# Selective scan with four states of 32 channels on the partitions, one broadcast of B for three groups, and part of the product with B on GpSimd

## The chip, the cores and the metric

One core of a Trainium2 chip. The metric is the device time of one launch in microseconds, and each kernel ran several times on the same chip as runs of the kernel before. A ratio here is the mean time of one kernel's fast runs over the mean of the other's fast runs of the same rounds, so it is not quite the ratio of the medians that are quoted beside it.

## The reference, cut to what matters

Four blocks work on images of 4 x 56 x 56 x 96. The first two contain a selective scan over the 3136 pixels of an image, in four directions, for 192 channels with 16 states each. The scans take nearly all of the time. Everything else (norms, projections, convolutions, attention, feed-forward) is called side work below, because the kernels run it beside the scans.

```python
dt = softplus(dt_raw @ dtw + dtb)            # (l, 192)
d_a = exp(dt[..., None] * a)                 # (l, 192, 16)
d_b = dt[..., None] * b_ssm[:, :, None, :]   # B is shared by the channels
h = d_a * h + d_b * x[..., None]             # the scan along l
y = einsum('bds,bs->bd', h, c_ssm)           # C is shared by the channels
```

## The kernel before

A direction's pixels are cut into 4 steps of 784 columns. That makes 2 layers x 4 images x 4 directions x 4 steps = 128 chunks. Before the change the 128 partitions hold 64 channels for two states, and a unit is one of 3 channel groups and one of 8 pairs of states. TensorE broadcasts B to the partitions into PSUM; VectorE multiplies dt*u by it **in place in PSUM** and scans; GpSimd multiplies by C; TensorE sums over the states.

```python
da = sp.tile([128, CS], F32, name="da", bufs=3)
nc.scalar.activation(da, ch.dt[g], AF.Exp, scale=ch.na[:, g, q : q + 1])
db = b                                              # B, broadcast, in PSUM
nc.vector.tensor_tensor(db, ch.du[g], db, ALU.mult)  # the product stays in PSUM
if n + 1 < len(units):
    b = self.spread_b(units[n + 1][0], units[n + 1][2])
...
hs = sp.tile([128, CS], F32, name="hs", bufs=2)
nc.vector.tensor_tensor_scan(
    hs[:, way], da[:, way], db[:, way], at if ch.step else 0.0, ALU.mult, ALU.add
)
...
hc = sp.tile([128, CS], F32, name="hc", bufs=2)
nc.gpsimd.tensor_tensor(hc, hs, ch.cc[q // 2][:, q % 2], ALU.mult)
```

The side work is written as generators from which the scan loop takes pieces at its yields. And the program text is not the order of the queues: a scheduler reorders the instructions of each engine at build time, by its own model of their durations, and each engine then works through its queue in that order.

## Time and profile before

| | before |
|---|---|
| time, median (range) | 12832 us (12782 to 12865, 4 runs of the comparison below) |
| TensorE / VectorE / GpSimd busy | 83% / 70% / 54% |
| scans, a unit | 1.84 us, never above 1.850 us |
| read and written by the DMA queue | 654 MB, 20.6% of the engines' time |

The lines themselves, and the pace of a unit worked out from them, are in the prediction. An engine whose work for one unit is far shorter than the pace is waiting for something.

### The profile page before, as it was taken

The page shows a single profiled execution, that of the slowest core. Times are in us where ns is not written, and L with a number is a line of the kernel's source. Part 1 is how long each engine was busy: PE and PEld are TensorE (multiplying, and loading weights), DVE is VectorE, ACT ScalarE, POOL GpSimd, SP SyncE. Part 2 cuts the span into 40 slices and gives each one's busy share as a digit, 9 for nine tenths or more (in the row PEclk, how much of TensorE's full clock was granted, in tenths as well). Part 3 has the DMA queues.
Part 4 walks back from the last instruction along what each step waited for, and adds up shares of the span by engine and source line. Part 5 has one row for each costly group of instructions (what it writes and reads, how often), then busy time and mean ns, then how long its engine had stood idle before and what let it go on. Part 6 is the DMA issues. An engine that isn't in the chain of part 4 may idle for free. (4 is left out here: it accounts for less than half of the span.)

```text
span 12868.3 us, 101763 instructions
## 1 busy us (share of the span) xinstructions
PE 10724.2 (83%) x32510; PEld 3416.3 (27%) x32510; DVE 9010.8 (70%) x7546; ACT 6582.8 (51%) x10422; POOL 6985.7 (54%) x3964
## 2 busy tenths in 40 slices
PE   7888888987789878897889888888888888888786
PEld 3222122222223122231223223321233213332143
DVE  4776777667776777767776666877668776777722
ACT  4655555555555555555555544445444454445511
POOL 4555656556554665546555555556555565555510
PEclk6766667766667667776767677766777667776665
DMA  3221212112211221212222121211212122211110
GB/s 84 61 59 46 69 45 54 49 41 68 57 48 50 57 67 42 57 44 65 50 54 53 37 68 49 52 45 41 62 49 52 41 50 61 51 43 40 41 33 28
DMA packets 233374, 662.64 MB, mean 51 GB/s; under 512 B 60866, under 2 KB 141252, under 8 KB 231204
## 3 DMA queue, kind: packets, MB, share of 16 engines
q1 hardware_dynamic: 232064, 654.32, 20.6%
q8 instruction: 257, 4.21, 0.1%
q14 instruction: 281, 2.30, 0.1%
q10 hardware_dynamic: 772, 1.80, 0.1%
HBM read 548.41 MB, written 107.58 MB: 51 GB/s over the span
## 5 line engine op out<-in xcount | busy, mean ns | idle before, releaser
L537 POOL TENSOR_TENSOR hc<-hs,cc 128x784 f32<-128x784 f32 x3072 | 5704.9, 1870 | 4545.8 <-DVE hs L531 3550.0
L551 PE MATMUL y<-hc,two 128*64 128x392 f32 x12288 | 4120.3, 740 | 1294.4 <-POOL hc L537 1219.0
L524 DVE TENSOR_TENSOR b<-du,b 128x784 f32<-128x784 f32 x3072 | 2963.4, 970 | 2481.5 <-PE b L483 2468.6
L531 DVE TENSOR_TENSOR_SCAN hs<-da,carry,b 128x784 f32<-128x784 f32 x2304 | 4166.1, 1834 | 149.4 <-ACT da L522 91.7
L522 ACT ACTIVATE da<-dt,na 128x784 f32<-128x784 f32 x3072 | 2862.0, 945 | 728.9 <-DVE hs L531 714.1
L483 PE MATMUL b<-bc,sel 96*128 96x512 bf16 (+1 forms) x6144 | 2110.7, 436 | 489.9 <-DVE hs L531 486.3
L551 PEld LDWEIGHTS y<-hc,two 128*64 128x64 f32 x12288 | 839.8, 178 | 3117.3 <-POOL hc L537 2320.1
L535 ACT COPY carry<-hs 128x1 f32<-128x1 f32 x2304 | 431.8, 189 | 2140.9 <-DVE hs L531 2134.1
L531 DVE TENSOR_TENSOR_SCAN hs<-da,b 128x784 f32<-128x784 f32 x768 | 1346.3, 1774 | 54.4 <-ACT da L522 21.5
L483 PEld LDWEIGHTS <-sel 96*128 96x128 bf16 x6144 | 457.7, 108 | 3176.4 <-DVE hs L531 1322.1
L431 PE MATMUL ps<-U,wd 64*108 64x392 f32 (+1 forms) x1536 | 864.0, 774 | 0.0
L461 POOL TENSOR_TENSOR du<-dt,U 128x784 f32<-128x784 f32 x384 | 783.0, 2047 | 147.0 <-ACT dt L456 138.9
L593 POOL TENSOR_TENSOR rs<-rs,power 112x4 f32<-112x4 f32 x252 | 257.4, 1021 | 964.6 <-ACT rs L592 784.8
L455 PE MATMUL ps<-dtr,wd 12*128 12x392 f32 (+1 forms) x1536 | 752.5, 736 | 9.4 <-ACT dt L456 3.6
L652 PE MATMUL ps<-win,dg 64*64 64x220 f32 (+9 forms) x2016 | 689.5, 496 | 0.0
L522 ACT ACT_TABLE_LOAD x511 | 655.6, 1283 | 8.3
L568 ACT COPY Ya<-y 64x392 f32<-64x392 f32 x512 | 348.3, 680 | 550.8 <-PE y L565 476.6
L596 PE MATMUL ps<-ident,rs 112*96 112x112 f32 x2016 | 423.6, 376 | 202.8 <-POOL rs L593 202.0
L456 ACT ACTIVATE dt<-ps,wd 128x392 f32<-128x392 f32 x768 | 426.8, 585 | 288.8 <-PE ps L455 279.7
L456 ACT ACT_TABLE_LOAD x339 | 434.9, 1283 | 78.9 <-PE ps L455 73.7
L596 PEld LDWEIGHTS ps<-ident,rs 112*96 112x96 f32 x2016 | 349.2, 250 | 395.4 <-POOL rs L593 308.0
L652 PEld LDWEIGHTS ps<-win,dg 64*64 64x64 f32 (+2 forms) x2016 | 337.1, 175 | 353.9 <-issue 258.7
(215 smaller groups left out, 6739.9 us busy)
## 6 DMA issues: line engine op xcount, KB each, us to landing
cc<-cd SPq DMA_DIRECT2D x1024, 392.0 KB, 5.2
U<-u SPq DMA_DIRECT2D x64, 588.0 KB, 7.9
u<-w SPq DMA_DIRECT2D x56, 224.0 KB, 2.8
z<-w SPq DMA_DIRECT2D x56, 224.0 KB, 2.7
y<-Ya SPq DMA_DIRECT2D x8, 1568.0 KB, 7.0
w<-y SPq DMA_DIRECT2D x56, 224.0 KB, 3.9
w<-z SPq DMA_DIRECT2D x56, 224.0 KB, 4.0
wd<-in_wd_dram SPq DMA_DIRECT2D x32, 367.5 KB, 3.5
```

Of the source, the lines that this page charges most:

```text
L431: nc.tensor.matmul(ps[:m, :HC].rearrange("p (a b) -> p a b", b=HS), self.wx[rows, g, :m], self.in_order(self.U[rows, g], orient, c * CS + ...
L455: nc.tensor.matmul(ps[:, :HC], wt[rows, g], dtr[rows], start=True, stop=True)
L456: nc.scalar.activation(dt[:, h * HC : (h + 1) * HC], ps[:, :HC], AF.Softplus, bias=dtb[:, g : g + 1])
L461: nc.gpsimd.tensor_tensor(du.rearrange("p (a b) -> p a b", b=HS), ch.dt[g].rearrange("p (a b) -> p a b", b=HS), self.in_order(self.U[:, g] ...
L483: self.nc.tensor.matmul(ps[:, s], w, ch.bc[:, s], start=True, stop=True)
L522: nc.scalar.activation(da, ch.dt[g], AF.Exp, scale=ch.na[:, g, q : q + 1])
L524: nc.vector.tensor_tensor(db, ch.du[g], db, ALU.mult)
L531: nc.vector.tensor_tensor_scan(hs[:, way], da[:, way], db[:, way], at if ch.step else 0.0, ALU.mult, ALU.add)
L537: nc.gpsimd.tensor_tensor(hc, hs, ch.cc[q // 2][:, q % 2], ALU.mult)
L551: nc.tensor.matmul(self.y[64 * h : 64 * h + 64, :HC], self.two, hc[:, h * HC : (h + 1) * HC], start=q == 0, stop=False,)
L596: nc.tensor.matmul(ps[:, b], rs[:, q : q + 1].to_broadcast([NT, C]), self.ident[:NT, :NT], start=True, stop=True)
L652: self.nc.tensor.matmul(o[:, a - r0 : e - r0, x0:x1], diag[:, tap], win[:, a + dy - lo : e + dy - lo, x0 + dx : x1 + dx], start=n == 0, st ...
```

## The change

The intent: with four states of 32 channels on the partitions, one broadcast of B serves three channel groups, which relieves TensorE, the fullest engine. One of the three products with B goes from VectorE to GpSimd, and the product with C becomes one wide instruction. Since a channel's dt must now stand on four partition blocks, dt and dt*u are written to DRAM and read back four times.

```diff
@@ spread: new @@
+        for n, l in ((0, ch.dt), (1, ch.du)):
+            t = self.sp.tile([128, NG, CS], F32, name="dt" if n == 0 else "du")
+            for s in range(4):
+                self.nc.sync.dma_start(
+                    t[32 * s : 32 * s + 32], ch.dd[e][n].rearrange("(g d) t -> d g t", d=32)
+                )
+            l.append(t)
@@ spread_b: f32, one for three groups, and a copy to SBUF for GpSimd @@
+        ps = self.psum.tile([128, 2, 512], F32, tag="b", name="b", bufs=1)
+        for h in range(2):
+            nc.tensor.matmul(ps[:, h, :HC], self.sel[:, h, q], ch.cf, start=True, stop=True)
+        b = self.sp.tile([128, CS], F32, name="bs", bufs=1)
+        nc.scalar.copy(b.rearrange("p (h t) -> p h t", h=2), ps[:, :, :HC])
@@ begin(n): the third group's product with B, a round ahead @@
+            b, bs = self.spread_b(ch, q)
+            v = sp.tile([128, NG, CS], F32, name="v", bufs=3)
+            nc.gpsimd.tensor_tensor(v[:, 2], ch.du[e][:, 2], bs, ALU.mult)
@@ a round @@
-            db = b
-            nc.vector.tensor_tensor(db, ch.du[g], db, ALU.mult)
+                if g < 2:
+                    nc.vector.tensor_tensor(
+                        v[:, g].rearrange("p (h t) -> p h t", h=2),
+                        ch.du[e][:, g].rearrange("p (h t) -> p h t", h=2), b, ALU.mult,
+                    )
+            if n + 1 < len(rounds):
+                nxt = begin(n + 1)
...
-            nc.vector.tensor_tensor_scan(
-                hs[:, way], da[:, way], db[:, way], at if ch.step else 0.0, ALU.mult, ALU.add
-            )
+            for g in range(NG):
+                nc.vector.tensor_tensor_scan(
+                    v[:, g, way], das[g][:, way], v[:, g, way], at[:, g : g + 1] if ch.step else 0.0, ALU.mult, ALU.add
+                )
...
-            nc.gpsimd.tensor_tensor(hc, hs, ch.cc[q // 2][:, q % 2], ALU.mult)
+            nc.gpsimd.tensor_tensor(v, v, cc.unsqueeze(1).to_broadcast([128, NG, CS]), ALU.mult)
```

Cut: the new layout of the parameters, the projections (a third fewer matmuls), the sums over four states in column blocks of 32, the convolutions split into pieces of three taps, and tile counts. A chunk now has 8 rounds (2 halves of 96 channels x 4 groups of states), numbered 0 to 7 below; there are 1024 rounds.

## The prediction

> **What bounds the kernel now.** I read the page's busy shares first, then the costliest groups and the waits.
>
> ```profile
> PE 10724.2 (83%) x32510; PEld 3416.3 (27%) x32510; DVE 9010.8 (70%) x7546; ACT 6582.8 (51%) x10422; POOL 6985.7 (54%) x3964
> ...
> L537 POOL TENSOR_TENSOR hc<-hs,cc 128x784 f32<-128x784 f32 x3072 | 5704.9, 1870 | 4545.8 <-DVE hs L531 3550.0
> L551 PE MATMUL y<-hc,two 128*64 128x392 f32 x12288 | 4120.3, 740 | 1294.4 <-POOL hc L537 1219.0
> L524 DVE TENSOR_TENSOR b<-du,b 128x784 f32<-128x784 f32 x3072 | 2963.4, 970 | 2481.5 <-PE b L483 2468.6
> L531 DVE TENSOR_TENSOR_SCAN hs<-da,carry,b 128x784 f32<-128x784 f32 x2304 | 4166.1, 1834 | 149.4 <-ACT da L522 91.7
> ```
>
> There are 3072 units (128 chunks x 24), each one product with B, one scan, one product with C. TensorE is the fullest engine. VectorE, next in line, is idle for 2481 us before its product with B, nearly all of it for the broadcast of B out of TensorE (2468.6). So TensorE's in-order stream paces VectorE. The chain of waits that ended last covers too little of the span to say more. In the table by stage, the stretch from 150 to 12275 us holds the scans (6908 us of GpSimd, 8885 us of VectorE); 150 us lie before it and 593 us after it. A unit thus takes 12125 / 3072 = 3.95 us, three units 11.84 us.
>
> The third view decides this case: least, median and greatest duration of single lines of VectorE.
>
> ```profile
> L531 DVE TENSOR_TENSOR_SCAN hs<-da,carry,b x2304: 1811/1839/1850, 235.2 to 12272.6; 128x784 f32<-128x784 f32 x192
> L815 DVE TENSOR_TENSOR w<-w,ps x28: 591/618/619, 7594.1 to 12564.8; 96x448 f32<-96x448 f32 x28
> L862 DVE TENSOR_TENSOR w<-w,yq x56: 587/610/2991, 8031.0 to 12863.1; 96x448 f32<-96x448 f32 x56
> L818 DVE SCALAR_TENSOR_TENSOR w<-w,c,win x28: 654/656/4555, 7596.3 to 12565.5; 96x448 f32<-96x448 f32 x28
> ```
>
> The scan now reads one operand from SBUF (da) and one from PSUM (the product with B stays in its PSUM bank): it never varies. L815 also has a PSUM operand, and never varies. L862 and L818 read two tensors from SBUF, and are stretched up to sevenfold. The timeline around the longest:
>
> ```profile
> 11051.87 1.01 POOL L593 TENSOR_TENSOR rs<-rs,power 112x4 f32<-112x4 f32 x1 [5.12 <-ACT rs L592]
> 11052.45 4.55 DVE L818 SCALAR_TENSOR_TENSOR w<-w,c,win 96x448 f32<-96x448 f32 x1
> 11052.84 3.68 POOL L537 TENSOR_TENSOR hc<-hs,cc 128x784 f32<-128x784 f32 x2
> ```
>
> VectorE began at 11052.45 while GpSimd worked, and ended at 11057.00, 0.48 us after GpSimd's third instruction (11056.52). So a 0.66 us instruction sat out two whole products with C. GpSimd kept the resource from one instruction to the next.
>
> **What the Trainium skill says.** "SBUF — State Buffer", section "Who interferes with whom": a VectorE instruction with two SBUF inputs contends with a GpSimd instruction that reads SBUF; whoever comes first has the shared port for the whole instruction. The trace agrees (4.55 against 0.66 us; and one-SBUF-input scans at 1850 ns at most). "GPSIMD Engine Reference", section 3.1 gives 4497 ns for a two-input product of 2048 columns; the trace has 1862 ns (median) for 784, so the slope is (4497 - 1862) / 1264 = 2.085 ns a column. "TensorE: Matmul & The Clock Gate", Part 3, says matmuls with disjoint 32-column outputs run side by side; the trace has this for two of 64 (12288 at a mean of 740 ns are 4120 us busy, 335 each).
>
> **The change, part by part.** A round is now three units that share one B: 1024 rounds.
>
> TensorE is relieved. Broadcast: two f32 matmuls of 392 columns a round, against six bf16 ones (2680 us by the groups with shapes kept apart, busy union 2111). A 392-column f32 matmul takes about 0.75 us, so 1024 x 2 x 0.75 = 1536 us. Summing over states: 6 matmuls of 32 outputs a round, three side by side, 2 x 0.7 us a round: about 1430 us against 4120. Projections and step sizes: a third of the instructions, saving about 1000 us. TensorE falls from 10.7 to about 6.5 ms and no longer paces anything.
>
> VectorE: one of three products with B goes, 1024 x 0.97 = -990 us; some 140 us of remainders for the bf16 split go too. ScalarE: +1024 copies of B to SBUF at some 0.9 us (two of 392 columns take 0.47 each), minus two of three carry copies (-290 us), minus a third of the softplus and several casts: about level, 51% today, not a bound. DMA: dt and dt*u spread over DRAM, 128 chunks x 16 transfers x 301 KB = 616 MB on top of 663. At today's 20.6% share for 654 MB that makes some 40%; a transfer of 392 KB lands in 5.2 us, and each spread has two to three rounds of over 10 us: hidden.
>
> The part that costs: the product with B now lands in an SBUF tile v, because GpSimd cannot use PSUM and v is later multiplied whole. So **the scan reads da and v, two SBUF tensors**, and falls into the class of L862 and L818. GpSimd's reads and all scans then take turns. What needs the port, per round:
> - Product with C, now one instruction of 2352 columns: 1.862 + 1568 x 0.002085 = 5.13 us (an estimate with the page's slope; by three of today's it would be 5.59).
> - Product of one group with B on GpSimd: 784 columns, 1.86 us.
> - dt*u: 256 at 2.047 us (L461, 384 today) = 524 us, 0.51 a round. The small powers (L593): 252 x 1.02 us, some 0.22 a round within the scans.
> - Three scans: (4166 + 1346) us of both scan rows / 3072 = 1.79 each, 5.38 us.
> - VectorE's other instructions with two SBUF inputs, or of the 16-bit kind that L853 and L854 show stretched as well: at their medians about 0.18 ms, 0.18 a round.
>
> Sum: 5.13 + 1.86 + 0.51 + 0.22 + 5.38 + 0.18 = 13.3 us. The two products left on VectorE (1.94 us) have a PSUM input and run beside the product with C. I add 0.5 us a round for moments when neither holds the port: VectorE's side instructions that lie between scans (about 0.25 ms in all) and its waits for side chains (100 to 147 us for each of five lines in the list of waits: L797, L809, L686, L888, L845), some now on the path. Handing over is about even: a released VectorE instruction ends 0.48 us after GpSimd where it takes 0.61 to 0.66 alone, and GpSimd starts 0.14 us after a scan ends.
>
> 13.8 us x 1024 = 14.13 ms, plus 0.15 ms ahead and 0.59 ms behind, which hardly change: 14.87 ms. I say 14800 us, 15% slower, though VectorE and TensorE both have less to do.
>
> **The rivals.**
> 1. No lock for scans: the engines overlap as before. Then VectorE has 1024 x (1.94 + 5.38) + 570 us of the rest = 8.1 ms and GpSimd 1024 x 7.0 + 0.75 ms = 7.9 ms, nearly balanced, TensorE out of the way: with a tenth of waits and 0.74 ms of ends some 9.3 to 9.9 ms, 25% faster. This is what the change aims at. Against it: every line with two SBUF inputs in the trace shows stretched cases, including plain float ones. For it: no scan with two SBUF inputs exists in this trace, and a scan takes 2.3 ns a column, so it might leave the port free half of the time.
> 2. A partial lock, with the port shared by columns or released between scans in a useful way: something between, 11 to 12.7 ms. Against it: the 4.55 us case is whole instructions, and both orders show it: in the timeline the product with C that starts at 11208.30, 0.22 us behind an L862, takes 2.13 us against a median of 1.86.
> 3. Lock plus convoys: GpSimd's in-order queue holds powers and dt*u that wait for ScalarE (today 785 us for L592) while a scan waits behind the port; or the spread through DRAM arrives late at the chunk's start. Each 1 us a round is 1.0 ms: 15.5 to 16.5 ms. For it: nothing overlaps any more, so side waits count. Against it: TensorE has slack now, so side chains get shorter.
>
> **Range and chances.** The mechanism is the large doubt, its size the small one. Given the lock, the sum runs from 13.8 (no extra, cheap handovers) to 15.6 ms (5.59 us products with C, 1.3 us lost a round). No lock or a weak one: 8% together for faster. Between them, 3%. Slower: 89%. Range 13800 to 15700.
>
> **What would show it.** Right: scans with a mean well over 1.84 us, up to some 7 or 8 us for the first scan of a round, or with medians unchanged but long maxima; GpSimd and VectorE hardly ever at work together save in the products with B; the wide product with C near 5.1 us when it isn't blocked; TensorE under 60% busy and no wait for L483's successor worth a millisecond; DMA landing well ahead of use. Wrong: scans steady at 1.84 us with GpSimd busy beside them, and a span under 10 ms (rival 1); a wide product near 5.6 us; ScalarE or the spread named as the releaser of the scans (rival 3).

## The result, and the profile after

After: 16251 us median (16239 to 16265, 4 runs), before: 12832 us. Ratio 1.267 (95% interval 1.262 to 1.272): slower, by more than the range allowed.

The page of the kernel after: busy time of each engine, and groups by line (busy us, mean ns of one, idle time before them and its releaser).

```profile
PE 9331.0 (57%) x28926; PEld 3524.1 (22%) x28926; DVE 12472.7 (77%) x6273; ACT 5527.1 (34%) x7879; POOL 9309.0 (57%) x2680
...
L560 DVE TENSOR_TENSOR_SCAN v<-da,carry,v 128x784 f32<-128x784 f32 x2304 | 7524.0, 3315 | 175.3 <-ACT da L548 149.0
L568 POOL TENSOR_TENSOR v<-v,cc 128x2352 f32<-128x2352 f32 x1024 | 5923.6, 5786 | 352.1 <-ACT carry L566 226.0
```

TensorE was relieved as intended and is no longer the fullest engine. But a scan takes 3315 ns in the mean instead of 1834. Single lines of the kernel after, least / median / greatest duration in ns:

```profile
L560 DVE TENSOR_TENSOR_SCAN v<-da,carry,v x2304: 1812/1840/11820, 262.4 to 15622.2; 128x784 f32<-128x784 f32 x192
L568 POOL TENSOR_TENSOR v<-v,cc x1024: 5122/5160/11188, 156.9 to 15624.1; 128x2352 f32<-128x2352 f32 x171
L551 DVE TENSOR_TENSOR v<-du,b x2048: 934/961/973, 149.7 to 15608.1; 128x784 f32<-128x784 f32 x187
```

The scan's median is unchanged and its greatest value is over six times that; the product with B on VectorE, which has one input in PSUM, never varies. The timeline of one round shows how the two engines stand in each other's way (start, duration, engine, line):

```profile
7211.55 1.85 DVE L551 TENSOR_TENSOR v<-du,b 128x784 f32<-128x784 f32 x2 [1.81 <-ACT bs L485]
...
7213.32 10.10 DVE L560 TENSOR_TENSOR_SCAN v<-da,v 128x784 f32<-128x784 f32 x3
7213.46 6.63 POOL L568 TENSOR_TENSOR v<-v,cc 128x2352 f32<-128x2352 f32 x1
```

Three scans that take 5.3 us alone took 10.10, and the product with C took 6.63 instead of 5.16. The sum of the four alone would be 10.5 us: they ran one after the other. Taken singly in the trace, the scans are 1.83, 6.67 and 1.76 us long. The product with C started during the first and ended 4.94 us after it. The second scan started when the first ended and was done only 1.65 us after the product with C.

How far does this explain the time? From the starts and ends in the trace I took, within the stretch of the scans (15472 us), the time in which an instruction of GpSimd or a scan of VectorE is open, and the rest. The port is the access to SBUF for which the two engines take turns (see the prediction); an instruction that has started and waits for it counts as open.

| stage of the scans | after | a round |
|---|---|---|
| GpSimd's instruction or a scan open | 12900 us | 12.6 us (the prediction's sum: 13.3) |
| neither | 2572 us | 2.5 us (the prediction: 0.5) |

(The prediction's 13.3 holds 0.18 us of VectorE's other instructions, which are not counted here.) So the lock, that is the taking of turns, cost about what was predicted, even a little less, and the excess over the prediction is idle time that was to be 0.5 us a round. It isn't even over the rounds. The gap between the starts of successive products with C, median over 128 chunks, from round r to r+1:

| r | 0 | 1 | 2 | 3 | 4 | 5 | 6 | 7 |
|---|---|---|---|---|---|---|---|---|
| after, us | 14.2 | **20.2** | 14.0 | 11.7 | 11.9 | 12.7 | 13.4 | 13.9 |

One gap in each chunk is 8 us too long (its mean, 25.1 us, is longer still). The timeline of the kernel after around such a gap:

```profile
1917.81 11.72 DVE L560 TENSOR_TENSOR_SCAN v<-da,carry,v 128x784 f32<-128x784 f32 x3
1917.89 6.71 POOL L568 TENSOR_TENSOR v<-v,cc 128x2352 f32<-128x2352 f32 x1
...
1924.55 3.33 POOL L521 TENSOR_TENSOR v<-du,bs 128x784 f32<-128x784 f32 x1
...
1929.45 1.82 DVE L551 TENSOR_TENSOR v<-du,b 128x784 f32<-128x784 f32 x2
...
1931.42 2.95 PE L483 MATMUL b<-cf,sel 128*128 128x392 f32 x4 [3.94 <-DVE v L551]
1934.47 0.81 ACT L485 COPY bs<-b 128x784 f32<-128x784 f32 x1 [3.95 <-PE b L483]
...
1935.36 2.81 POOL L521 TENSOR_TENSOR v<-du,bs 128x784 f32<-128x784 f32 x1 [7.47 <-DMA U<-u]
...
1938.13 5.14 POOL L568 TENSOR_TENSOR v<-v,cc 128x2352 f32<-128x2352 f32 x1
```

The scans that the product with C at 1938.13 needs ended at 1929.53. But in GpSimd's queue two products with B (L521) stand before it. The second waits for a copy of B (1934.47), that for a broadcast (1931.42), that for the PSUM tile to come free (VectorE's products at 1929.45). GpSimd is idle for 7.47 us, and for the last 5.8 of them the product with C was ready behind the head of its queue. (The view names a transfer as the releaser because that came last by its record; the chain just read goes through the copy.)

### The profile page after: what moved, and what is told of

The parts are those of the page before. It is cut to its first block, busy times and chain, and to the rows that moved or that the text cites. A ratio compares the mean times of both kernels' runs of the same rounds, so it can differ in the third digit from the quotient of the medians.

```text
span 16237.4 us, 95405 instructions
## 1 busy us (share of the span) xinstructions
PE 9331.0 (57%) x28926; PEld 3524.1 (22%) x28926; DVE 12472.7 (77%) x6273; ACT 5527.1 (34%) x7879; POOL 9309.0 (57%) x2680
## 3 DMA queue, kind: packets, MB, share of 16 engines
q1 hardware_dynamic: 631424, 1399.75, 34.5%
## 5 line engine op out<-in xcount | busy, mean ns | idle before, releaser
L560 DVE TENSOR_TENSOR_SCAN v<-da,carry,v 128x784 f32<-128x784 f32 x2304 | 7524.0, 3315 | 175.3 <-ACT da L548 149.0
L568 POOL TENSOR_TENSOR v<-v,cc 128x2352 f32<-128x2352 f32 x1024 | 5923.6, 5786 | 352.1 <-ACT carry L566 226.0
L521 POOL TENSOR_TENSOR v<-du,bs 128x784 f32<-128x784 f32 x1024 | 2358.3, 2303 | 4048.4 <-ACT bs L485 2819.8
L583 PE MATMUL y<-v,four 128*32 128x392 f32 x12288 | 2753.2, 756 | 2864.4 <-POOL v L568 2247.9
L483 PE MATMUL b<-cf,sel 128*128 128x392 f32 x4096 | 2612.6, 780 | 2507.0 <-DVE v L551 2506.2
L551 DVE TENSOR_TENSOR v<-du,b 128x784 f32<-128x784 f32 x2048 | 1884.9, 959 | 1616.8 <-ACT bs L485 727.9
L560 DVE TENSOR_TENSOR_SCAN v<-da,v 128x784 f32<-128x784 f32 x768 | 2516.9, 3326 | 73.4 <-ACT da L548 73.4
L483 PEld LDWEIGHTS b<-cf,sel 128*128 128x128 f32 x4096 | 1066.4, 286 | 4074.0 <-issue 3817.9
L485 ACT COPY bs<-b 128x784 f32<-128x784 f32 x1024 | 822.3, 803 | 1087.7 <-PE b L483 1062.5
L453 POOL TENSOR_TENSOR duc<-dtc,U 96x784 f32<-96x784 f32 x256 | 669.8, 2616 | 662.4 <-ACT dtc L443 448.4
```

What stands on the lines that cost most here:

```text
L453: nc.gpsimd.tensor_tensor(du.rearrange("p (a b) -> p a b", b=HS), ch.dtc[e].rearrange("p (a b) -> p a b", b=HS), self.in_order(self.U[e], ...
L483: nc.tensor.matmul(ps[:, h, :HC], self.sel[:, h, q], ch.cf, start=True, stop=True)
L485: nc.scalar.copy(b.rearrange("p (h t) -> p h t", h=2), ps[:, :, :HC])
L521: nc.gpsimd.tensor_tensor(v[:, 2], ch.du[e][:, 2], bs, ALU.mult)
L551: nc.vector.tensor_tensor(v[:, g].rearrange("p (h t) -> p h t", h=2), ch.du[e][:, g].rearrange("p (h t) -> p h t", h=2), b, ALU.mult,)
L560: nc.vector.tensor_tensor_scan(v[:, g, way], das[g][:, way], v[:, g, way], at[:, g : g + 1] if ch.step else 0.0, ALU.mult, ALU.add)
```

## The experiments

Three theories of the result were at stake from the start: the lock (the scan's second operand in SBUF), the convoys (side chains in GpSimd's queue), and, against the prediction's word "hidden", the spread through DRAM. In the diffs "kernel after" is the base unless another is named; they are cut, and some draw several lines together. Six runs compute something else on purpose (e6, e10, e11, e13, e15, e18). They passed the comparison with the reference all the same; its tolerance evidently doesn't see what they leave out, so they count only for their times, and passing does not by itself prove the other runs right.

### e1 and e2: only the operand's place

```diff
+  p = self.psum.tile([128, 1024], F32, tag="p", name="p", bufs=1)[:, :CS]   # e1
+  p = sp.tile([128, CS], F32, name="p", bufs=1)                             # e2
   nc.vector.tensor_tensor(p, ch.du[e][:, g], b, ALU.mult)     # all three groups on VectorE
-  nc.vector.tensor_tensor_scan(v[:, g, way], das[g][:, way], v[:, g, way], ...)
+  nc.vector.tensor_tensor_scan(v[:, g, way], das[g][:, way], p[:, way], ...)
   # no copy of B; convolutions whole and two ps tiles instead of four, to make room in PSUM
```

> Keeps four states of 32 channels, the single broadcast of B and the spread via DRAM; all three products with B go back to VectorE and land in a PSUM tile p, so the scan reads da (SBUF) and p (PSUM); to have two banks for p the convolutions run whole again and the shared PSUM tile has 2 buffers. Lock theory: no scan over 1.85 us, GpSimd and scans overlap, a round is VectorE's own 3 x 0.96 + 3 x 1.79 + some 0.6 us of side work = 8.9 us, with a tenth of waits 9.5: 9.8 to 10.8 ms in all. Rival (the loss is side chains, in-order queues or late transfers, not the port): stays over 14 ms, scans may still be steady. Rival no-lock with slow scans: scans slower than 1.85 us here too.

> The same as e1_product_psum in every instruction, but p is an SBUF tile, so the scan reads two SBUF tensors. Lock theory: product with C 5.16 + three scans 5.4 + the two products with B that lie between scans 1.9 + powers and dt*u 0.75 + about 1 us of waits = 14.2 us a round, 14.2 to 16 ms in all; scans up to over 5 us long. If the place of the operand does not matter: the same time as e1 within 2%.

Measured: e1 14189 us (ratio to before 1.106), e2 16555 us (1.290). The single lines of e1:

```profile
L557 DVE TENSOR_TENSOR_SCAN v<-da,carry,p x2304: 1830/1846/1850, 256.8 to 13580.3; 128x784 f32<-128x784 f32 x192
L565 POOL TENSOR_TENSOR v<-v,cc x1024: 5128/5161/5327, 160.5 to 13582.4; 128x2352 f32<-128x2352 f32 x171
```

and of e2:

```profile
L557 DVE TENSOR_TENSOR_SCAN v<-da,carry,p x2304: 1832/1851/11427, 275.9 to 15947.2; 128x784 f32<-128x784 f32 x192
```

The two kernels differ in where one tile lies. With it in PSUM no scan is ever stretched, with it in SBUF one takes up to 11.4 us, and the time differs by 2.37 ms. That shows the lock. The order of the queues, which matters below, can hardly be the cause here: in the traces 0.99 of VectorE's first 4000 instructions and 0.98 of GpSimd's instructions stand in the same sequence in both (TensorE 0.92, ScalarE 0.98), and the durations of the scans sum to 5.63 ms in e1 and to 8.15 ms in e2, a rise of 2.5 ms, as large as that of the whole time. But e1 was not the fast kernel that the removal of the lock promised (9.8 to 10.8 ms), and e2 too lies above its range. The median round of e1 is 10.1 us, its mean 13.1. The groups of e1 name a wait of 1909 us of VectorE for the broadcast of B, and the timeline shows one:

```profile
6015.04 12.09 PE L676 MATMUL ps<-win,dg 128*128 128x448 f32 x54
...
6027.06 0.93 PE L483 MATMUL b<-cf,sel 128*128 128x392 f32 x2
...
6028.02 0.98 DVE L551 TENSOR_TENSOR p<-du,b 128x784 f32<-128x784 f32 x1 [12.61 <-PE b L483]
```

54 matmuls of a convolution stood in TensorE's queue ahead of two that broadcast B, with a single buffer for it.

### e3: the control for the two

```diff
-  name="ps", bufs=4
+  name="ps", bufs=2
   # convolutions whole again, as in the kernel before
```

> The changed kernel with one part undone: convolutions in one piece, side work paced as before, 2 buffers of the shared PSUM tile in place of 4. It is the base of e1 and e2. Theory: the port and the waits stay, 16.0 to 16.6 ms. If the splitting of side work were the cause of the loss: over 3% faster; if two PSUM buffers throttle side chains that are on the path now: 2 to 5% slower.

Measured: 16713 us (1.303), 0.46 ms or 2.8% above the kernel after, in the range expected if fewer PSUM tiles hold side chains up. So part of the loss in e1 and e2 is their price for PSUM: the splitting of the convolutions and the larger number of PSUM tiles, which the change brought along, are together worth that much.

### e4 and e8: other ways to ease the port

e4 leaves v in SBUF and takes the third product with B and the copy of B away from GpSimd and ScalarE. e8 goes back to PSUM with half tiles, so that convolutions may stay split, and places the preparation as e5 below does.

```diff
-  if g < 2:
       nc.vector.tensor_tensor(v[:, g], ch.du[e][:, g], b, ALU.mult)    # e4: for all three
-  nc.gpsimd.tensor_tensor(v[:, 2], ch.du[e][:, 2], bs, ALU.mult)
```

```diff
+  for h in (1, 0) if ch.rev else (0, 1):                               # e8: half by half
+      p = self.psum.tile([128, 512], F32, tag="p", name="p", bufs=1)[:, :HC]
+      nc.vector.tensor_tensor(p, ch.du[e][:, g, s], b[h], ALU.mult)
+      nc.vector.tensor_tensor_scan(v[:, g, s][:, way], das[g][:, s][:, way], p[:, way], first, ...)
```

> The changed kernel with one part undone: the third group's product with B moves from GpSimd back to VectorE (PSUM operand, result still in v), and the copy of B to SBUF goes. VectorE gets 0.96 us a round more. Lock theory: GpSimd needs the port 1.88 us a round less and the wait for the copy of B goes (about 0.5 us a round), while the added product runs beside the product with C: minus 1.9 to 2.5 ms, 13.7 to 14.4 ms. If VectorE's own work were the bound: plus 1.0 ms, 17.2 ms.

> Product with B on VectorE into a PSUM tile of half a chunk (one bank), so that B's broadcast has two independent halves, three buffers of the shared PSUM tile stay and convolutions stay split; the preparation placed as in e5_prep_early. Scans in halves of 392. No scan reads two SBUF tensors. Port-free theory: VectorE 6 x (0.56 + 0.98 + 0.1) = 9.9 us a round, side stalls shorter than in e1: 10.5 to 11.5 us a round, 11.5 to 12.5 ms, faster than before. If side work stalls the single broadcast as in e1 (3 us a round over its 10.1 us floor): 13.5 to 14.2 ms.

Measured: e4 14297 us (1.114), e8 13990 us (1.090). Moving work off GpSimd pays though VectorE is the busier engine, which fits a product that has an input in PSUM and needs no port there: 1.95 ms for 1024 moved products. Part of that is the long gap: from round 1 to 2 the median is 10.7 us in e4 and the mean 18.2, against 20.2 and 25.1 in the kernel after. e8 is the fastest version found (e14 below, at 13969 us, is level with it). It missed the 11.5 to 12.5 ms expected of a kernel free of the port and lies where side work that stalls the broadcast was to put it; e4 is in its expected range. None beats the kernel before.

### e5 and e7: is it the convoys?

e5 projects the next chunk and computes its dt two rounds earlier, and dt*u one round later; e7 takes all side work of a stage in one burst, so that most rounds have none.

```diff
-  if r == 3: project_step   elif r == 4: step_sizes, times_u(0)   elif r == 5: spread(0), times_u(1)
+  if r == 1: project_step   elif r == 2: step_sizes   elif r == 5: times_u(0), spread(0)   elif r == 6: times_u(1)
```

```diff
-  if u >= UNITS - LAST:
-      due = 10**6
+  due = 10**6 if u >= 3 else 0
```

> The changed kernel; only the rounds of a chunk in which the next chunk's preparation is issued differ: projections in round 1 in place of 3, softplus in round 2 in place of 4, dt*u in rounds 5 and 6 in place of 4 and 5. In the changed kernel's trace the second product with C of a chunk to the third takes 25.1 us on the mean against 12 to 17 for the others, as dt*u stands in GpSimd's queue and waits up to 14 us for softplus. Convoy theory: that stall goes, minus 0.7 to 1.4 ms, 14.9 to 15.6 ms, the port sum unchanged. If the stall is only moved (the port or ScalarE's order make it): within 2% of 16.25 ms.

> The changed kernel with the other layers' work not spread between scans but issued in one burst at the start of each of the eight stages; correct. The rest of a stage is scans alone. In that part a round should take the port's sum without powers: 5.16 + 1.86 + 5.4 + 0.5 (dt*u) = 12.9 us plus the preparation stall of about 1.4 us: 13.9 to 14.5 us, if side work costs the changed kernel its last us a round; 15 us if side work costs nothing. In all slower than the changed kernel or level, as the burst stands alone.

Measured: e5 15900 us (1.238), only 0.35 ms less, and the median gap from round 1 to 2 is still 20.3 us. e7 17639 us (1.374, two runs): slower, but 961 of its gaps have no side work in them and these show the gap from round 1 to 2 at 20.15 us in the mean of 128 chunks. So neither the place of the preparation nor the side work makes this gap.

### e6: no spread at all

```diff
+  if ch.c or ch.l or ch.i or ch.orient or ch.rev:          # every chunk but the first
+      ch.dt.append(self.kept[0][e]); ch.du.append(self.kept[1][e]); return
```

> Wrong on purpose: dt and dt*u are read back from DRAM and spread for the first chunk alone, all later chunks use those tiles; everything else is issued as before, the writes to DRAM too. Takes away 616 MB and the waits for landing. If the spread via DRAM is hidden: minus 0.1 to 0.4 ms (waits for dt and du transfers add to about 0.7 ms over three engines, partly in parallel). If transfers are a main part of the loss: minus over 1 ms.

Measured: 14571 us (1.135), 1.68 ms less. The expectation was missed by far: the gap is gone (median 11.9 us) and "neither" fell from 2572 to 969 us. The spread, called hidden in the prediction, is somehow behind most of the excess. But how? It reads back 606 MB, it makes every chunk wait for a landing, and the scheduler orders the queues around it.

### e9, e10, e11: queue order, traffic, waits

The order of GpSimd's queue can be read from the built program. In the kernel after, one product with B is ahead of the product with C at rounds 0 and 1 of nearly all chunks, and **two at round 2, in 128 chunks of 128**: the step from one to two is the gap. (In e6 there is such a step in 15 chunks.)

```diff
+  with self.tc.issue_after(hcs[n - 2].ins) if n >= 2 else nullcontext():   # e9: order only
       nc.gpsimd.tensor_tensor(v[:, 2], ch.du[e][:, 2], bs, ALU.mult)
```

```diff
+  t[32 * s : 32 * s + 32, :, w], ch.dd[e][n]...[:, :, w]    # e10: w = 8 of 784 columns, after the first chunk
```

```diff
+  l.append(t if first else (self.head.dt, self.head.du)[n][0])   # e11: lands in a tile that nothing reads
```

> Correct. Same instructions as the changed kernel and the same transfers; only an order is forced on GpSimd: the product with B of round n waits its turn until GpSimd has issued the product with C of round n-2. In the changed kernel as built, GpSimd's queue has one product with B ahead of the product with C at rounds 0 and 1 of a chunk and two at round 2, in 128 of 128 chunks; with the edge it has one, everywhere. Theory Q (queue order: at round 2 the product with C stands behind the product with B of round 4, which needs round 3's products, a broadcast and a copy first): the gap between the products with C of rounds 1 and 2 falls from a median of 20.2 us to 12 to 14 us, and the total by 7 us x 128 = 0.9 ms or somewhat more: 15.0 to 15.4 ms. Theory T (the traffic of the spread through DRAM holds back the rows of C in the transfer queue): 16.0 to 16.3 ms, gap still near 20 us. Theory D (the chunk waits for its spread to land): the same as T.

> Wrong result on purpose: after the first chunk the spread of dt and dt*u reads only 8 of 784 columns back from DRAM, into the tiles of the first chunk, so nearly all of the traffic goes and every wait for a landing stays. The order of GpSimd's queue moves too: two products with B ahead of the product with C at round 2 in 70 chunks (55 of them... stepping up there), at round 0 in 50, at round 7 in 66. Theory Q: 15.2 to 16.2 ms, with gaps of 18 to 20 us wherever the count of products ahead steps from one to two. Theory T: 14.5 to 14.9 ms, as with no spread at all (14.57), and no gaps. Theory D: 16.0 ms or more only if the latency of a small transfer matters; else as T.

> Wrong result on purpose: every transfer of the spread runs in full, but after the first half chunk it lands in tiles that nothing reads, and all rounds read the first half chunk's dt and dt*u. So the traffic stays and no round waits for a landing. GpSimd's queue has two products with B ahead of the product with C at round 2 in 128 of 128 chunks, as in the changed kernel, and again at round 7 in 115. Theory Q: the gap at round 1 to 2 stays near 20 us and the total is 15.6 to 16.6 ms. Theory T: 15.8 to 16.3 ms, because the traffic is all there. Theory D: 14.5 to 14.9 ms, gap gone. With the two other runs of this set: Q alone says low, middle, high; T says high, low, high; D says high, low or middle, low.

Measured: e9 15968 us (1.243), e10 15108 us (1.176), e11 15772 us (1.228). In e9 the median gap fell from 20.2 to 11.9 us, which shows what made it in most chunks; its mean fell only from 25.1 to 19.0. And the total fell by 0.28 ms, not 0.9: gaps at rounds 4 and 5 grew. e10 and e11 said that the traffic costs more (1.14 ms) than the waits (0.48), which no theory had foreseen, and in both the queues' order had moved too.

A second trait of the order came out of the traces. Side instructions of VectorE and GpSimd between two products with C, mean count per round: 3.27 from round 1 to 2 in the kernel after, 0.2 to 1.6 elsewhere; in e6 0.9 to 1.5 everywhere. It looks as if the scheduler heaps side work where it expects the scans to wait for the spread. The timeline of the kernel after in such a heap:

```profile
2676.36 5.32 DVE L560 TENSOR_TENSOR_SCAN v<-da,carry,v 128x784 f32<-128x784 f32 x3
...
2680.69 1.80 POOL L619 TENSOR_TENSOR rs<-rs,power 112x4 f32<-112x4 f32 x1 [7.64 <-ACT rs L618]
...
2687.07 1.83 POOL L453 TENSOR_TENSOR duc<-dtc,U 96x784 f32<-96x784 f32 x1 [4.58 <-ACT dtc L443]
...
2698.52 1.01 POOL L619 TENSOR_TENSOR rs<-rs,power 112x4 f32<-112x4 f32 x1 [9.62 <-ACT rs L618]
2699.49 1.84 POOL L521 TENSOR_TENSOR v<-du,bs 128x784 f32<-128x784 f32 x1
```

From 2681.68, when the scans end, to 2699.49, 17.8 us, GpSimd and VectorE do nothing but side work and preparation, and mostly wait for it: a small instruction at the head of the queue waits for ScalarE, with the product with B behind it.

### e12 to e14: the order of two queues held

```diff
+  tc.add_manual_dep(i, main[m - 1].ins.name, edge)       # side instruction i of round m: not before round m-1
+  tc.add_manual_dep(main[m + 1].ins, i.name, edge)       # and not after round m+1; with e9's edge
```

e13 is e12 with few columns; e14 is e8 with these edges.

> Correct. The forced order of e9 (the product with B of round n behind the product with C of round n-2), and the side work that runs beside the scans (convolutions, norms, projections) held in place: on GpSimd and on VectorE each of its instructions is queued not before the main instruction of the round before, and not after that of the round after, the one in which it is written. In the changed kernel as run, side instructions on the two engines came to 3.27 between the products with C of rounds 1 and 2 of a chunk (mean over 128 chunks) and to 0.2 to 1.6 at the others; with the edges VectorE's queue has 0.6 to 1.1 at each round but the last. All transfers of the spread and all waits for them stay. Theory O (the spread through DRAM costs time by the static order that it makes the scheduler choose: the step in the count of products ahead, and the side work put in a heap at the chunk's start, where the scheduler expects a wait for the spread): rounds without side work 12.6 to 13.2 us, and the excess of the rounds with it falls from 1.6 ms to about 0.9 ms, as without a spread: 14.5 to 15.3 ms. Theory T (traffic in the DMA engines or in SBUF): 15.6 to 16.1 ms, as with the first edge alone (15.97). Theory H (the edges take away freedom that the two queues need): above 16.1 ms.

> Wrong result on purpose: the paced kernel with only 8 of 784 columns read back from DRAM after the first chunk. The order of the two queues is now nearly the same with and without the traffic (one product with B ahead in both; side instructions in VectorE's queue at rounds 0 to 3 are 0.94, 1.03, 1.09, 0.52 against 0.91, 0.98, 1.06, 0.68). Theory O: within 0.3 ms of the paced kernel. Theory T: lower than the paced kernel by 0.8 ms or more, near 14.6 to 15.1 ms.

> Correct. The kernel of e8 (the product with B in half tiles in PSUM, all on VectorE; 13.99 ms, rounds of 10.4 us in the median and 12.9 us in the mean) with its side work held in place by the same edges. If heaps of side work are what lifts its mean over its median, 1 us a round or more comes back: 12.5 to 13.2 ms, about the kernel before. If it is each side instruction's own chain of waits that costs, heaped or not: 13.7 to 14.3 ms.

Measured: e12 15664 us (1.219), e13 14897 us (1.160), e14 13969 us (1.088). e12 is lower than e9 by 0.30 ms, less than expected, and e13 lower than e12 by 0.77 ms. Taken alone that speaks for the traffic, as theory T had it. e14 gained nothing over e8: there it isn't heaps.

### e15, e16: traffic or late landing

```diff
   # e15: e12 with e11's unread landing
+  if r == 1: project_step   elif r == 2: step_sizes, times_u(0)   elif r == 4: spread(0), times_u(1)   # e16, on e12
```

> Wrong result on purpose: the paced kernel of e12 in which every transfer of the spread runs in full but, after the first half chunk, lands in tiles that nothing reads (as in e11). The forced order of GpSimd's and VectorE's queues is that of e12 nearly to the count. So the traffic of e12 stays and its waits for the landing go. Theory L (latency: each chunk waits once for the last of its spread's transfers; reading 8 columns lands some 4 to 7 us sooner, and 0.77 ms over 128 chunks is 6.0 us a chunk): 14.6 to 15.0 ms, as with few columns or below. Theory T (the traffic itself: 35.7% of the DMA engines' time against 19.0%, or SBUF's writes): 15.4 to 15.7 ms, as in e12.

> Correct. The paced kernel with each chunk's preparation moved forward: projection in round 1 of the chunk before, step sizes and dt*u of the first half in round 2, its spread in round 4 (as soon as the tile it overwrites is free), instead of rounds 3, 4 and 5. Nothing is left out. Theory L: the landing is then ahead of its use by a round or more and most of the 0.77 ms comes back: 14.8 to 15.2 ms. Theory T: the traffic is as before, 15.5 to 15.8 ms.

Measured: e15 15453 us (1.204), e16 15481 us (1.206). Without its waits, or with the transfers issued earlier, the spread still cost 0.6 ms over e13. By this the traffic was the cause. But the durations denied it: scans had a mean of 3227 ns in e12 and 3243 in e13, and no transfer landed later in a way that mattered (rows of C: 2.5 against 2.4 us). And a comparison of the built queues showed that only two of the five had been held: of the first 4000 instructions of ScalarE, 0.77 stood in the same sequence in e12 and e13, and 0.65 in e15 and e13.

### e17, e18: all five queues held

The order of TensorE, VectorE, ScalarE, GpSimd and the queue that issues the transfers was read out of e13's build and put into two other kernels as ordering edges, 39 thousand instructions, alike one by one but for 56 memsets. The traces confirm it: leaving out memsets and table loads, TensorE's, ScalarE's and GpSimd's instructions stand in one and the same order in e13, e17 and e18, and VectorE's in all but 6 of 6266 places.

```diff
+  for a, b in zip(at, at[1:]):                            # at: e13's order of this engine's instructions
+      tc.add_manual_dep(own[b], own[a].name, edge)        # order only, no wait is added or removed
```

> Correct: the changed kernel with all its transfers and all its waits, but with the order of the instructions on all five queues (TensorE, VectorE, ScalarE, GpSimd, and the queue that issues the transfers) forced to be that of e13, the one with few columns (read out of that build and put in as ordering edges; it is the same instruction for instruction but for 56 memsets on GpSimd). e12 and e13 had nearly the same order on VectorE and GpSimd alone; on ScalarE only about 0.77 of the first 4000 instructions stood in the same sequence, and 0.85 on TensorE. Theory O (static order of all queues is the cost, the traffic itself is hidden): 14.8 to 15.1 ms, as e13 (14.90). Theory T (traffic or late landing): 15.4 to 15.8 ms, as e12 (15.66).

> Wrong result on purpose: as e17, but the spread lands in tiles that nothing reads after the first half chunk (as in e11 and e15): all of the traffic, none of its waits, at e13's order of all five queues. Theory O: as e13, 14.8 to 15.1 ms. Theory T in the form of traffic: 15.3 to 15.6 ms, as e15 (15.45). Theory T in the form of late landing: 14.8 to 15.0 here and 15.4 to 15.8 in e17, so the difference of the two runs is what the waits cost.

Measured:

| at e13's order | traffic | waits for it | us | ratio to before |
|---|---|---|---|---|
| e13 | no | yes (of 8 columns) | 14897 | 1.160 |
| e18 | yes | no | 14893 | 1.163 |
| e17, correct, nothing left out | yes | yes | 14988 | 1.170 |

The DMA queues of e13:

```profile
q1 hardware_dynamic: 631424, 794.25, 19.0%
```

and of e18 (packets, MB, share of the DMA engines' time):

```profile
q1 hardware_dynamic: 631424, 1399.75, 37.4%
```

606 MB more, and no time beyond the noise: the medians are level, the ratios 0.3% apart. e18 lacks the short waits that e13 has, so the traffic alone could cost a little; but traffic and waits together, e17 against e13, cost 0.09 ms by the medians and 0.14 by the ratios. **The same kernel, with all its instructions, transfers and waits, is 1.26 ms faster when only the order of its queues is another** (16251 to 14988). The waits of the kernel after (engine, line, what it waited for: us in total, times, longest):

```profile
POOL v L521 <- ACT bs L485: 2819.8, 486, 15.0
POOL rs L619 <- ACT rs L618: 1693.9, 199, 27.5
DVE v L551 <- ACT bs L485: 727.9, 287, 11.4
POOL duc L453 <- ACT dtc L443: 448.4, 68, 18.7
```

and of e17:

```profile
POOL v L533 <- ACT bs L497: 1663.2, 442, 14.6
POOL rs L631 <- ACT rs L630: 924.9, 113, 28.7
DVE v L563 <- ACT bs L497: 520.8, 197, 13.5
POOL duc L465 <- ACT dtc L455: 198.4, 46, 13.8
```

Nearly the same heads of queues wait in both, for less in e17. The time with neither engine at work is 1349 us in e17 against 2572, a difference of 1.22 ms, nearly the whole gain; time with one of them at work is 12880 against 12900. So the order changes the idle part and leaves the time of the lock as it was.

## Why the prediction was wrong

Point by point, by its own steps:

- **The mechanism: right.** The scan with two SBUF inputs and GpSimd's reads take turns. Shown by the pair e1 and e2 (2.37 ms for one operand's place), and by single scans of up to 11.8 us beside products with C.
- **Sizes of the port's users: right.** The product with C was put at 5.13 us and takes 5.16 (median). The sum of 13.3 us a round came out as 12.6. The hand-over is somewhat cheaper than a sum of whole instructions: in the timeline above 10.10 us against 10.5.
- **TensorE relieved, VectorE and TensorE no bound: right.** TensorE is at 57% and 9331 us. The prediction's 6.5 ms was too low because it counted each f32 matmul once, where the traces have two records of some 0.75 us each: the broadcast has 4096 records and 2613 us (put at 1536), the sum over the states 12288 records and 2753 us (put at 1430). TensorE did not become the bound, but GpSimd's product waits for a copy of this broadcast (2.95 us of TensorE in the timeline of the long gap); what the longer broadcast costs there was not tested. ScalarE, put at about level, fell from 6583 to 5527 us.
- **The failed step: "I add 0.5 us a round for moments when neither holds the port."** It was 2.5 us. The term of 0.5 ms became 2.57 ms. One sign of it was written down: "no wait for L483's successor worth a millisecond". GpSimd waits 2820 us for the copy of the broadcast. With the port sum's error of -0.7 ms this makes up the difference: 14.87 - 0.7 + 2.1 = 16.3 ms.
- **Within it, the spread "hidden": right of the transfers, wrong of the kernel.** At one order the transfers cost nothing that can be told from noise (e18), and with their waits about 0.1 ms (e17). (The added volume was 745 MB, not 616, as the writes to DRAM were left out; the queue's share is 34.5%.) But the scheduler, whose order changes when they shrink (e12 against e13, where they also land in other tiles), chose an order around them that cost 1.26 ms over another order of the same instructions. e12, which holds the queues of VectorE and GpSimd, got 0.59 ms of it. What those edges take away is the step from one product ahead to two and the side work heaped at the chunk's start. The rest came only in e17, when e13's order was put on all five. That is mostly a change of ScalarE's order (a quarter of its first 4000 instructions) and TensorE's, but GpSimd's (0.92 in the same sequence in the traces of e12 and e13) and VectorE's (0.98) change a little too. Which of these instructions matter was not tried.
- **Rival 3 named the wait but not its cause.** It had "GpSimd's in-order queue holds powers and dt*u that wait for ScalarE", which the list of waits shows (1694 us for the powers), and its range of 15.5 to 16.5 ms holds the result. It blamed the lock for making side waits count, and a late spread; e17 shows that 1.22 of the 2.06 ms by which the idle time exceeds its 0.5 us a round go with the order alone.
- **The upper end of the range was added up too low.** Its own terms, 5.59 us products with C and 1.3 us lost, give 13.74 + 1.3 = 15.04 us a round, and with 0.74 ms at the ends 16.1 ms, not 15.6. Even so it stays below the result.
- **What remains.** Even at the better order 1.3 us a round are idle, where 0.5 were put. The list of waits names side chains and the copy of B on which GpSimd's product waits (1663 us in e17, part of it hidden); no run takes these away one by one, so this is read, not shown. With 1.3 the prediction's sum is 13.3 + 1.3 = 14.6 us a round and 15.7 ms; with the port's measured 12.6 it is 13.9 us and 15.0 ms, which is e17.

What stays open: how much of the order's cost is due to which queue; what share of the gain came over TensorE's granted clock, which was 0.66 in the kernel after and 0.69 in e17; and whether the scheduler's order for the kernel after is bad because its model of the transfers is off or because it lacks the lock in its model. No run tells these apart.

## What to carry to other kernels

An operand that moves from PSUM to SBUF can cost more than the instructions that the move saves, when VectorE then reads two SBUF tensors beside a busy GpSimd: count such instructions of both engines into one sum. When an experiment that takes a transfer away saves time, compare the built queues before blaming the transfer, and repeat it with their order held: here the traffic seemed to cost 0.77 ms and, with its waits, cost about 0.1 ms at a held order. And where engines work in order, ask what stands ahead of the critical instruction in each queue; a wait of 10 us for an instruction of 1 us is invisible in shares of busy time.

## What the Trainium skill lacked or had wrong

- "SBUF — State Buffer", section "Who interferes with whom", does not name the scan in its list of operations that take the shared ports; only its general rule for two SBUF inputs covers it. The scan does contend with two SBUF inputs: up to 11.4 us (e2) against at most 1.850 us with one input in PSUM (e1).
- The same section says "for the whole instruction" of the modes in which VectorE uses both ports; for two SBUF inputs only the page's summary says that the second to issue is blocked until the first finishes. The runs agree for the scan (6.67 us behind a product with C), but hand-overs overlap a little: 10.10 us for four instructions whose durations alone sum to 10.5. The page doesn't say so.
- Not lacking but borne out: its statement that DMA never contends with a compute engine. 606 MB more in the same queue order took no time beyond the noise (14893 against 14897 us).
- "GPSIMD Engine Reference", section 3.1 times one size of a two-input instruction, an addition, beside a rate of about 2.6 cycles an element; it has no time of a product. The prediction took the time for a product's, and the slope worked out from it held at another size: 5.13 us estimated, 5.16 measured for 2352 columns.
- No page tells that the order in which a scheduler puts the same instructions in their queues can be worth 8% of a kernel (16251 against 14988 us), or that shrinking a transfer changes that order on every engine (e12 and e13, the first 4000 instructions in the traces: 0.75 of ScalarE's to 0.98 of VectorE's in the same sequence).
